# A third level of seven-product multiplication in more pairs of steps, and mixed kernels spread otherwise, in a fused AdaLN and FFN kernel

## The chip, the cores and the metric

One Trainium2 chip; the kernel runs on 1 of its cores. The metric is the device time of one execution in microseconds. Before the change: 2576.84 us, the median of three runs (2576.32 to 2578.92).

## The reference

All arrays are float32. x is (32, 128, 2048). Two blocks follow each other:

```
agg_w[b] = sum_k att[b,k] * weight[k]          # 32 mixed kernels of 128 x 128, att from a small MLP and a softmax
h   = agg_w[b] @ x[b] + agg_b[b]               # for every sample b
x1  = x + h @ W.T + bias + low-rank update     # W is 2048 x 2048, the update 16 experts of rank 16
y   = grouped conv of x1 along L (9 taps, 4 groups of 32 channels) + context + bias
t   = y[:, perm] in 16 heads of 128
out = x1 + (gelu(t @ up) @ down)[:, unperm]    # per head 128 -> 512 -> 128
```

What the change touches is the large product, x (4096 rows of 2048) by W (with the low-rank update added into it), and the 32 mixed kernels, which are made beside it on VectorE.

## The kernel before

The engines are named as in the profile: PE does matmuls, DVE is VectorE, ACT ScalarE, POOL GpSimd, and SP issues most DMAs.

**Three levels of seven products.** The large product is split into 2 x 2 blocks three times in the manner of Strassen and Winograd: seven products of sums and differences in place of eight.

- The outer level is a loop of seven *rounds*, `ROUNDS = P1, P2, P6, P7, P5, P3, P4`. Each has its own weights: four blocks of W, or differences of them (`outer_weights`), brought in and combined on POOL while the round before runs. What a round yields is added into partial sums in DRAM that are loaded before and stored after a step (`ADDED`, `olds_load`, `part_store`).
- A round has eight *steps* g = 0 to 7, each 512 rows of x. `multiply` does the inner level: seven products P1 to P7, each of four matmuls of 128 x 128 by 512 columns. Their second weights t1, t2, t4 are made by `inner_weights` on POOL, at step 7 of the round before; the sums `s` of the input by `x_combine` on POOL, one step ahead.
- The third level works on *pairs* of steps (g, g + 1). In a pair listed in `PAIRS`, the inner products P2 and P4 of both steps (16 matmuls of 512 columns) are done together as seven *quarters* of four matmuls of 256 columns each: `multiply_third`. The differences of the weights come from `third_weights` (half on POOL at once, half as `quarter_ops` on DVE, one between two products), the sums of the inputs (tile `sq`) from `third_inputs`, four operations on POOL, or on DVE in round P6.
- In a pair listed in `MORE`, P3 and P7 are done the same way as a second family: `multiply_more`. Only P1, P5 and P6 stay as full products. A quarter of the second family needs two additions on DVE, of 512 and of 256 elements, where one of the first needs one. `more_weights` makes eight differences on POOL and eight (`more_ops`) on DVE, `more_inputs` four sums (tile `sv`) on POOL. In such a pair four quarters come in the even step and ten in the odd one; the odd step's order is P1, two quarters, P5, two, P6, two, two, P3's, P4's.

Before the change MORE has the middle pairs, steps 2 to 5, of rounds P7 and P3; PAIRS has all pairs but the first of P1, and in P4 the first alone.

**Order.** The program is scheduled by hand: each engine does its instructions in the order in which the code gives them. `between(j)` is called after each product and puts other work of DVE there: two operations of a mixed kernel (`mixed_kernel`, L714; eight make one 128 x 128 kernel), one quarter_op and one more_op. In rounds P2 to P3 each of the steps 1 to 6 makes one mixed kernel. In round P1 `w_make_two` makes W with its update, two of its 16 blocks ahead of each of the first six steps, and `row_sums` and `unsummed_first` add up rows of W on DVE. `small` is a generator with the small MLP, which goes on by a little after each step.

**Buffers.** All large tiles of 8 KB a partition share 26 slots (`SLOTS`), taken in the order of the code; a new tile waits until the last reader of the slot's old one is done. PSUM has eight banks, used in turn by hand (`bank`, `done`). After the seven rounds, and partly beside P4, come mixing, convolution and the heads' FFN, which the change does not touch.

Of the kernel before, what the change touches and what calls it, by code (L numbers as in the profile page):

```python
# [11 lines left out]
ALU = mybir.AluOpType  # L12
# [36 lines left out]


PAIRS = {
    "P1": (1, 2, 3), "P2": (0, 1, 2, 3), "P6": (0, 1, 2, 3), "P7": (0, 1, 2, 3),
    "P5": (0, 1, 2, 3), "P3": (0, 1, 2, 3), "P4": (0,),
}
MORE = {"P7": (1, 2), "P3": (1, 2)}
ENDS = ("P1", "P4")
EARLY = 2

# [2 lines left out]
def adaln_ffn_kernel(  # L61
# [355 lines left out]
    def in_pair(r, g):  # L417
        return g // 2 in PAIRS[r]

    rest = []  # L420

    def third_inputs(i, eng):

        (x11, x12), (x21, x22) = (
            [xa[n][:, 1, :, h * NQ : (h + 1) * NQ] for h in range(2)] for n in (i, i + 1)
        )
        tt = eng.tensor_tensor
        t = slot(f"sq_{i}", (P, 4, 2, NQ))
        tt(t[:, 0], x21, x22, ALU.add)
        tt(t[:, 1], t[:, 0], x11, ALU.subtract)  # L430
        rest.append((t[:, 2], x11, x21))
        rest.append((t[:, 3], x12, t[:, 1]))
        if eng is nc.gpsimd:
            sums_rest(eng)
        return {
            "P1": x11, "P2": x12, "P3": t[:, 3], "P4": x22,
            "P5": t[:, 0], "P6": t[:, 1], "P7": t[:, 2],
        }

    def sums_rest(eng):  # L440
        while rest:
            eng.tensor_tensor(*rest.pop(0), ALU.subtract)

    def more_weights(name, rhs):

# [33 lines left out]
    def in_more(r, g):  # L479
        return g // 2 in MORE.get(r, ())  # L480

    def multiply_more(r, g, lhs, rhs, accs, between, families):

        px, py = bank(), bank()
        if g % 2 == 0:
            both = [accs]
            held.extend((both, {}, {}))
        both, *sums = held
        if g % 2:
            both.append(accs)  # L490

        def add(ps, *to):
            for si, oi in to:
                for acc in accs:
                    nc.vector.tensor_tensor(acc[:, si, oi], ps, acc[:, si, oi], ALU.add)  # L495

        def product(k, ps, first, last):
            for kc in range(4):
                nc.tensor.matmul(  # L499
                    ps, lhsT=lhs[k][:, bass.ts(kc, P)], rhs=rhs[k][kc],  # L500
                    start=first and kc == 0, stop=last and kc == 3, skip_group_check=True,
                )

        def quarter(n, k):

            quarters, x = families[n]
            qs = sums[n]
            if k in ("P1", "P5", "P2"):
                qs[k] = bank()
            ps = qs[{"P6": "P1", "P7": "P1", "P4": "P1", "P3": "P5"}.get(k, k)]  # L510
            first, last = k in ("P1", "P2", "P5"), k in ("P2", "P3", "P4")
            for i, out in enumerate(halves(ps)):
                for kc in range(2):
                    nc.tensor.matmul(  # L514
                        out, lhsT=x[k][:, 1 - i if n else i, bass.ts(kc, P)],
                        rhs=quarters[i][k][kc],
                        start=first and i == 0 and kc == 0, stop=last and i == 1 and kc == 1,
                        skip_group_check=True,
                    )
            b, h = {  # L520
                "P1": (0, 0), "P2": (0, 0), "P6": (0, 1), "P5": (1, 1), "P7": (1, 1),
                "P3": (0, 1), "P4": (1, 0),
            }[k]
            cols = slice(h * NQ, (h + 1) * NQ)
            for acc in both[b]:
                part = acc[:, :, n, cols]
                nc.vector.tensor_tensor(  # L527
                    part, ps.rearrange("p (s n) -> p s n", s=2), part, ALU.add
                )
                if n:  # L530
                    part = acc[:, 1, 0, cols]
                    nc.vector.tensor_tensor(part, ps[:, NQ : 2 * NQ], part, ALU.add)
            if last:
                done(ps)

        def quarters_of(*nks):
            if g % 2:
                for n, k in nks:
                    quarter(n, k)

        product("P1", px, True, False)
        add(px, (0, 0))
        between(0)
        quarters_of((0, "P6"), (0, "P5"))
        product("P5", py, True, True)
        add(py, (1, 1), (0, 1))
        done(py)
        between(1)
        quarters_of((1, "P6"), (0, "P7"))
        product("P6", px, False, True)  # L550
        add(px, (0, 1), (1, 1), (1, 0))
        done(px)
        between(2)
        if g % 2 == 0:
            quarter(0, "P1")
            quarter(0, "P2")
            between(3)
            quarter(1, "P1")
            between(4)
            quarter(1, "P2")  # L560
            between(5)
            return
        quarters_of((1, "P5"), (0, "P3"))
        between(3)
        quarters_of((1, "P7"), (0, "P4"))
        between(4)
        quarters_of((1, "P3"))
        between(5)
        quarters_of((1, "P4"))
        held.clear()  # L570
        for b, accs in enumerate(both):
            for (_, new), acc in zip(ADDED[r], accs):
                part_store(new, g - 1 + b, acc, nc.sync)
# [648 lines left out]
    for i, (r, g) in enumerate(steps):  # L1222
        ri = i // NG
        last_round = ri + 1 == len(ROUNDS)
        if i + 1 < len(steps):
            if i + 1 not in xs:
                xs[i + 1] = x_loads(*steps[i + 1])
            if not last_round:
                lhs[i + 1] = x_combine(*steps[i + 1], xs.pop(i + 1))
                if g == 2 * PAIRS[r][0]:  # L1230
                    quarters, quarter_ops = third_weights(r, rhs)
                if in_pair(r, g) and g % 2 == 0 and g > 0 and r != "P6":
                    sq = third_inputs(i, nc.gpsimd)
                    if in_more(r, g):
                        sv = more_inputs(i)
                if r in MORE and g == 2 * MORE[r][0] - 1:
                    more, more_ops = more_weights(r, rhs)
        if i == 0:
# [48 lines left out]
        def between(j):  # L1287

            if j == 3 and 0 <= k_early < EARLY:
                outer_sums(k_early, early_x)  # L1290

            b = (ri - 1) * (NG - 2) + g + 1 if ri > 0 else g - (NG - 2)
            if (g in range(1, NG - 1) if ri > 0 else g >= NG - 2) and b < B:
                k = j - 2 if r == "P5" and g == 1 else j
                if 0 <= k < KEXP // 2:
                    mixed_kernel(b, (2 * k, 2 * k + 1))
            if ri == 0 and j == 2:
                for k in blocks[6 + 2 * g : 8 + 2 * g]:
                    wt[k] = w_load(*k)
            if j < 4 and quarter_ops:  # L1300
                nc.vector.tensor_tensor(*quarter_ops.pop(0), ALU.subtract)
            if j < 4 and more_ops:
                nc.vector.tensor_tensor(*more_ops.pop(0), ALU.subtract)
            if i == NG - 1 and j == 3:
                olds_load(i + 1)
            if j == 3 and ahead and steps[i + 2][0] == "P6":
                xs[i + 2] = x_loads(*steps[i + 2])
            if ri == 0 and j in (1, 3) and unsummed:
                row_sums(*unsummed.pop())
            if ri == 0 and j == 5 and unsummed_first:  # L1310
                t = unsummed_first.pop(0)
                tt = nc.vector.tensor_tensor
                tt(wsum[:, 0, 0], wsum[:, 0, 0], t[:, 0, 0], ALU.add)
                tt(wsum[:, 0], wsum[:, 0], t[:, 1], ALU.add)
            if last_round:
                if j == 1 and i + 1 < len(steps):
                    lhs[i + 1] = x_combine(*steps[i + 1], xs.pop(i + 1))
                    olds_load(i + 1)
                if j == 4 and i + 2 < len(steps):
                    xs[i + 2] = x_loads(*steps[i + 2])  # L1320
                if j in (2, 4):
                    stage(k0 + j // 2, stage_first)
                if j % 2:
                    stage_third(k0 + j // 2)
                else:
                    stage(k0 + j // 2, stage_second)
# [10 lines left out]
            multiply(r, g, lhs.pop(i), rhs, olds.pop(i), between)  # L1337
        xa.pop(i - 1, None)
        ss.pop(i - 1, None)
        if in_pair(r, g) and g % 2 == 0 and (g == 0 or r == "P6" or last_round):  # L1340
            sq = third_inputs(i, nc.gpsimd if r in ENDS else nc.vector)
        next(chain, None)
        if i > 4:
# [95 lines left out]
```

## Time and profile before

| | |
|---|---|
| median of the runs | 2576.84 us |
| the profiled execution's own time | 2577.27 us |
| its span, first to last instruction | 2575.5 us |
| PE busy | 2564.0 us |
| DVE busy | 1579.5 us, 2450 instructions |
| POOL busy | 1394.2 us, 1158 instructions |
| matmul records | 7142, two for each matmul |
| mean granted TensorE clock | 0.999 |

The views used: the page (busy times of the engines; the chain of work that ended last, followed back from the last instruction to whatever released each), that chain in order of time (start, length, what; "x56" are 56 records of one line in a row), tables of busy time in stretches of the span, and the instructions of one engine in order of time, with its idle time before and what ended it in brackets. A line such as L594 is a product in `multiply_third` (L357 in `multiply`, L499 in `multiply_more`), L607 and L514 are the quarters of the two; L714 is a mixed kernel's operation, L283 an outer sum on POOL. Tile names come without numbers: `xt` is an input of the large product, `P_t`, `P_q`, `P_v` weights of the inner level and of the third level's two families.

Rounds as seen on PE: P1 from 33 to 297 us (with the making of W), P2 to 483, P6 to 669, P7 to 853, P5 to 1039, P3 to 1223; then P4 with the rest.

### The profile page before, as it was taken

Reading aid. Unit: us, or ns where it says so; the run is one execution under the profiler, and the core shown is the slowest. Engines: PE = TensorE matmul, PEld = TensorE weight load, DVE = VectorE, ACT = ScalarE, POOL = GpSimd, SP = SyncE. Lnnn points to the kernel's source line nnn. Section 1 sums busy time; section 2 is a strip of 40 time slices with the busy share of each in tenths; the row PEclk is TensorE's granted clock in tenths of the full one; section 3 lists DMA queues with packets and bytes.
Section 4 is the critical chain, followed back from the end, with each engine's and each line's share of the span. In section 5 each row is a group of like instructions: output and inputs, shape, how many; then the busy total and the mean of one; then the engine's idle time right before and its main releaser. Section 6 shows DMA issues by size and latency. Waiting matters only on the chain.

```text
span 2575.5 us, 22121 instructions
## 1 busy us (share of the span) xinstructions
PE 2564.0 (100%) x7142; PEld 1355.4 (53%) x7142; DVE 1579.5 (61%) x2450; ACT 532.3 (21%) x1099; POOL 1394.2 (54%) x1158
## 2 busy tenths in 40 slices
PE   9999999999999999999999999999999999999999
PEld 4455555555566555566554554455555554455543
DVE  5665576666585576675476666666666666667611
ACT  0000000000000000000011244444444444444432
POOL 7431788878997736989432134444344434434222
PEclk9999999999999999999999999999999999999999
DMA  7452588579366486574866887787777877777432
GB/s 322 182 211 113 198 338 344 212 285 370 151 249 263 196 337 273 221 287 168 281 230 210 279 290 266 224 259 230 226 223 234 252 246 223 222 251 237 164 123 90
DMA packets 186867, 610.42 MB, mean 237 GB/s; under 512 B 17664, under 2 KB 91904, under 8 KB 142336
## 3 DMA queue, kind: packets, MB, share of 16 engines
q1 hardware_dynamic: 147936, 473.48, 51.2%
q0 software_dynamic: 32992, 132.14, 15.2%
q10 hardware_dynamic: 5824, 3.40, 0.5%
q8 instruction: 57, 0.93, 0.1%
q14 instruction: 58, 0.48, 0.1%
HBM read 372.45 MB, written 202.94 MB: 223 GB/s over the span
## 4 chain that ended last, share of the span: by engine, by line
PE 95%; DVE 3%; DMA 2%; issue 0%; SPq 0%; POOLq 0%; ACT 0%; ACTq 0%; DVEq 0%
PE bank L594 26%; PE bank L986 17%; PE bank L997 17%; PE bank L607 9%; PE bank L357 7%; PE bank L842 6%; PE bank L750 4%; PE bank L499 3%; PE bank L223 3%; PE bank L514 2%; DMA w<-in_WT 1%; DVE ags L714 1%; DMA xt<-in_xT 0%; DVE u L527 0%; DVE u L495 0%
## 5 line engine op out<-in xcount | busy, mean ns | idle before, releaser
L986 PE MATMUL bank<-t,ws 128*128 128x512 f32 x1024 | 460.3, 592 | 0.0
L997 PE MATMUL bank<-gl,ws 128*128 128x512 f32 x1024 | 460.1, 592 | 0.0
L1004 POOL DMA_INDIRECT out<-t,orow x128 | 152.3, 1189 | 535.8 <-DVE t L1002 452.5
L989 ACT ACTIVATE gl<-bank 128x512 f32<-128x512 f32 x512 | 306.1, 598 | 433.3 <-PE bank L986 414.1
L997 PEld LDWEIGHTS bank<-gl,ws 128*128 128x128 f32 x1024 | 194.6, 190 | 232.9 <-issue 231.5
L986 PEld LDWEIGHTS bank<-t,ws 128*128 128x128 f32 x1024 | 194.6, 190 | 226.6 <-issue 222.2
L594 PE MATMUL bank<-P_t,s_P 128*128 128x512 f32 x640 | 284.3, 592 | 0.4 <-ACT m_P L589 0.4
L1002 DVE TENSOR_TENSOR t<-bank,t 128x512 f32<-128x512 f32 x128 | 88.4, 690 | 320.2 <-PE bank L997 309.4
L735 POOL TENSOR_TENSOR x<-x,fb 128x512 f32<-128x512 f32 x128 | 174.5, 1392 | 198.9 <-DMA x<-in_x 136.4
L741 ACT ACTIVATE bank<-w,aggb 128x512 f32<-128x512 f32 x128 | 80.8, 684 | 880.3 <-DMA w<-w_d 867.8
L283 POOL TENSOR_TENSOR xt<-xt,xt 128x512 f32<-128x512 f32 x120 | 159.0, 1358 | 104.6 <-DMA xt<-in_xT 88.4
L714 DVE SCALAR_TENSOR_TENSOR ags<-mix,att_bc,ags 128x128 f32<-128x128 f32 x224 | 195.5, 873 | 4.7
L594 PEld LDWEIGHTS bank<-P_t,s_P 128*128 128x128 f32 x640 | 121.4, 190 | 140.4 <-issue 136.6
L587 DVE TENSOR_TENSOR u<-bank,u 128x512 f32<-128x512 f32 x156 | 101.6, 686 | 147.4 <-PE bank L594 135.1
L594 PE MATMUL bank<-wo_P,s_P 128*128 128x512 f32 x416 | 184.7, 592 | 0.0
L319 POOL TENSOR_TENSOR s_P<-xt 128x512 f32<-128x512 f32 x52 | 68.8, 1323 | 204.0 <-DMA xt<-in_xT 164.2
L970 POOL DMA_INDIRECT t<-hx_d,row x128 | 131.1, 1025 | 56.6 <-issue 25.6
L587 DVE TENSOR_TENSOR p<-bank,p 128x512 f32<-128x512 f32 x96 | 64.6, 687 | 117.8 <-PE bank L594 117.1
L594 PEld LDWEIGHTS bank<-wo_P,s_P 128*128 128x128 f32 x416 | 79.0, 190 | 89.2 <-issue 87.3
L842 PE MATMUL bank<-va,tw_l 128*128 128x256 f32 x512 | 121.5, 380 | 0.7 <-DVE va L826 0.7
L853 ACT ACTIVATE cv<-bank,ctxb 128x128 f32<-128x128 f32 x256 | 73.0, 368 | 234.6 <-PE bank L842 234.6
L753 DVE TENSOR_TENSOR x<-bank,x 128x512 f32<-128x512 f32 x128 | 88.1, 690 | 50.8 <-POOL x L735 21.9
(242 smaller groups left out, 3869.0 us busy)
## 6 DMA issues: line engine op xcount, KB each, us to landing
xt<-in_xT SPq DMA_DIRECT2D x84, 1024.0 KB
u<-u_d SPq DMA_DIRECT2D x40, 1024.0 KB
wo_P<-wb_d SPq DMA_DIRECT2D x36, 1024.0 KB
u<-c_d SPq DMA_DIRECT2D x64, 512.0 KB
x<-in_x SPq DMA_DIRECT2D x32, 1024.0 KB
xg<-x SPq DMA_DIRECT2D x256, 128.0 KB
hx_d<-x1t SPq DMA_DIRECT2D x32, 1024.0 KB
hx_d<-ht SPq DMA_DIRECT2D x32, 1024.0 KB
```

The costliest lines, as they stand in the source:

```text
L283: nc.gpsimd.tensor_tensor(out[:, i, j], a[:, i, j], b[:, i, j], op)
L357: nc.tensor.matmul(ps, lhsT=lhs[k][:, bass.ts(kc, P)], rhs=rhs[k][kc], start=first and kc == 0, stop=last and kc == 3, skip_group_check=True,)
L587: nc.vector.tensor_tensor(to, ps, to, ALU.add)
L594: nc.tensor.matmul(ps, lhsT=lhs[k][:, bass.ts(kc, P)], rhs=rhs[k][kc], start=first and kc == 0, stop=last and kc == 3, skip_group_check=True,)
L607: nc.tensor.matmul(out, lhsT=sq[k][:, i, bass.ts(kc, P)], rhs=quarters[i][k][kc], start=first and i == 0 and kc == 0, stop=last and i == 1 ...
L714: nc.vector.scalar_tensor_tensor(ag, mix[:, k], att, ag, ALU.mult, ALU.add)
L735: nc.gpsimd.tensor_tensor(xt[:, f], xt[:, f], late["fb"][:, f], ALU.add)
L842: nc.tensor.matmul(out, lhsT=w[:, 2 * i + r], rhs=rhs, start=first and r == 0, stop=last and r == 1, skip_group_check=True,)
L986: nc.tensor.matmul(pu, lhsT=w[:, m * P : (m + 1) * P], rhs=t[:, 0], start=True, stop=True)
L989: nc.scalar.activation(gl[m], pu, AF.Gelu)
L997: nc.tensor.matmul(pd, lhsT=w[:, (MC + m) * P : (MC + m + 1) * P], rhs=gl[m], start=(m == 0), stop=(m == MC - 1),)
L1004: nc.gpsimd.indirect_dma_start(out=out, out_offset=bass.IndirectOffsetOnAxis(ap=orow[:, g, h : h + 1], axis=0), in_=t[:, 1], in_offset=None,)
```

## The change

- `PAIRS`: P1's first pair gets the third level. So `third_weights` of P1 comes two steps sooner, and P1's steps 0 and 1 go through `multiply_third` in place of `multiply`. Its DVE part, `quarter_ops`, starts at step 1.
- `MORE`: round P6 gets the second family in steps 2 to 5, and P7 and P3 in their last pair too, steps 6 and 7.
- In P6 the sums `sq` of such a pair stay on DVE: two at the end of the even step, two after the first quarters of the odd one. `sums_rest` takes operations with their kind and a count.
- Mixed kernels: in the rounds of MORE their 48 operations are handed out over steps 1 to 7, one after each of the first four products in steps 2 and 4 and two in the others, in place of two in steps 1 to 6. The other rounds keep theirs.
- In round P1 the row sums of W are moved: one of the sums of step 1 to step 2, and those of the first four blocks from the ends of steps 0 to 3 to steps 2 (twice), 3 and 4.

```diff
 PAIRS = {
-    "P1": (1, 2, 3), "P2": (0, 1, 2, 3), "P6": (0, 1, 2, 3), "P7": (0, 1, 2, 3),
+    "P1": (0, 1, 2, 3), "P2": (0, 1, 2, 3), "P6": (0, 1, 2, 3), "P7": (0, 1, 2, 3),
     "P5": (0, 1, 2, 3), "P3": (0, 1, 2, 3), "P4": (0,),
 }
-MORE = {"P7": (1, 2), "P3": (1, 2)}
+MORE = {"P6": (1, 2), "P7": (1, 2, 3), "P3": (1, 2, 3)}
...
-    def third_inputs(i, eng):
+    def third_inputs(i, eng, later=False):
...
-        tt(t[:, 0], x21, x22, ALU.add)
-        tt(t[:, 1], t[:, 0], x11, ALU.subtract)
-        rest.append((t[:, 2], x11, x21))
-        rest.append((t[:, 3], x12, t[:, 1]))
+        rest.append((t[:, 0], x21, x22, ALU.add))
+        rest.append((t[:, 1], t[:, 0], x11, ALU.subtract))
+        if not later:
+            sums_rest(eng, 2)
+        rest.append((t[:, 2], x11, x21, ALU.subtract))
+        rest.append((t[:, 3], x12, t[:, 1], ALU.subtract))
...
-    def sums_rest(eng):
-        while rest:
-            eng.tensor_tensor(*rest.pop(0), ALU.subtract)
+    def sums_rest(eng, n=4):
+        for _ in range(min(n, len(rest))):
+            eng.tensor_tensor(*rest.pop(0))
...
         quarters_of((0, "P6"), (0, "P5"))
+        if g % 2:
+            sums_rest(nc.vector)
         product("P5", py, True, True)
...
+        if g == 0:
+            b = (ri - 1) * (NG - 2) + 2
+            mixes = [(b + n // KEXP, n % KEXP) for n in range((NG - 2) * KEXP)]
+            mixes = [m for m in mixes if m[0] < B]
...
-                if in_pair(r, g) and g % 2 == 0 and g > 0 and r != "P6":
-                    sq = third_inputs(i, nc.gpsimd)
-                    if in_more(r, g):
-                        sv = more_inputs(i)
+                if in_pair(r, g) and g % 2 == 0 and g > 0:
+                    if r != "P6":
+                        sq = third_inputs(i, nc.gpsimd)
+                    elif in_more(r, g):
+                        sq = third_inputs(i, nc.vector, True)
+                if in_more(r, g) and g % 2 == 0:
+                    sv = more_inputs(i)
...
-            if (g in range(1, NG - 1) if ri > 0 else g >= NG - 2) and b < B:
+            if (g in range(1, NG - 1) if ri > 0 else g >= NG - 2) and b < B and r not in MORE:
                 k = j - 2 if r == "P5" and g == 1 else j
                 if 0 <= k < KEXP // 2:
                     mixed_kernel(b, (2 * k, 2 * k + 1))
+            if r in MORE and 0 < g and j < 4:
+                for _ in range(1 if g in (2, 4) else 2):
+                    if mixes:
+                        b, k = mixes.pop(0)
+                        mixed_kernel(b, (k,))
...
-            if j < 4 and quarter_ops:
+            if i and j < 4 and quarter_ops:
...
-            if ri == 0 and j in (1, 3) and unsummed:
+            if ri == 0 and unsummed and (j in (1, 3) and (i, j) != (1, 3) or (i, j) == (2, 4)):
                 row_sums(*unsummed.pop())
-            if ri == 0 and j == 5 and unsummed_first:
+            if (i, j) in ((2, 0), (2, 5), (3, 0), (4, 0)) and unsummed_first:
...
-        if in_pair(r, g) and g % 2 == 0 and (g == 0 or r == "P6" or last_round):
+        if in_more(r, g) and r == "P6":
+            sums_rest(nc.vector, 2)
+        elif in_pair(r, g) and g % 2 == 0 and (g == 0 or r == "P6" or last_round):
             sq = third_inputs(i, nc.gpsimd if r in ENDS else nc.vector)
```

## The prediction

> **What bounds the kernel now.** I read the page first (busy times, then the chain that ended last), then the chain in order of time for what a product costs, then a table of busy times by stretches, then the instructions of DVE and POOL in time.
>
> ```profile
> PE 2564.0 (100%) x7142; PEld 1355.4 (53%) x7142; DVE 1579.5 (61%) x2450; ACT 532.3 (21%) x1099; POOL 1394.2 (54%) x1158
> ...
> PE 95%; DVE 3%; DMA 2%; issue 0%; SPq 0%; POOLq 0%; ACT 0%; ACTq 0%; DVEq 0%
> ```
>
> PE has work in 2564.0 of 2575.5 us and makes up 95% of the chain: a matmul taken away shortens the program by its own time, unless something else is then late. So I need the price of a product and a list of what may be late.
>
> ```profile
> 82.11 24.03 PE bank L357 x56
> ...
> 220.25 17.17 PE bank L594 x40
> 237.41 12.10 PE bank L607 x56
> ...
> 762.10 10.30 PE bank L499 x24
> 772.40 6.91 PE bank L514 x32
> ```
>
> This is the chain in order of time (start, length, what). Each product is two records. 56 records with 512 columns take 24.03 us, 0.429 us each; 56 records with 256 columns take 12.10 us, 0.216 us each. Half the columns cost half, with the weight load hidden both times.
>
> [...]
>
> **PE: what goes.** A plain pair of steps is 2 x 24.03 = 48.06 us. A pair with the third level on P2 and P4 is 2 x 17.17 + 12.10 = 46.44 us: 16 full products became 28 halves. A pair with the third level on P3 and P7 as well is 44.77 us when nothing waits (762.10 to 806.87 in the same chain). So P1's first pair gives 1.62 us, and each of the four new pairs (two of P6, the last of P7 and of P3) gives 1.67 us: 1.62 + 4 x 1.67 = 8.3 us. The instructions to check it by: 5 x 12 products more, so 7142 + 120 = 7262 matmul records.
>
> **DVE: what the new pairs add.** Seven more additions of 512 (0.6 us apart) and seven of 256 (0.33 us apart) in each of the four pairs, 6.5 us a pair; in P6 also 8 differences of 256 for the weights. The waits that exist are in such pairs:
>
> ```profile
> core 0: us, PE busy (x) PEld busy (x) DVE busy (x) ACT busy (x) POOL busy (x), PEclk, DMA share, GB/s
> ...
> 576.50:622.90 46.40, 46.40 (x137) 25.84 (x136) 29.36 (x39) 0.00 (x0) 39.02 (x32) 1.00 0.94 364
> ...
> 715.80:761.90 46.10, 45.25 (x161) 30.21 (x160) 43.06 (x53) 0.00 (x0) 45.47 (x37) 1.00 0.63 254
> 761.90:806.70 44.80, 44.80 (x161) 30.41 (x161) 30.04 (x49) 0.00 (x0) 35.74 (x30) 1.00 0.73 284
> ```
>
> These are P6's third pair and P7's second and third. The second pair of P7 lasts 46.1 us and not 44.8: DVE is busy in 43.06 of it. The chain shows how a wait is made:
>
> ```profile
> 757.81 1.30 DVE ags L714
> 759.11 0.60 DVE u L527
> 759.72 0.34 DVE u L532
> 760.06 0.04 issue
> 760.10 1.99 PE bank L514 x8
> ```
>
> The last quarter, P4, adds into the bank that P7's quarter used; P7's additions (L527, L532) stand on DVE behind two operations of a mixed kernel (L714), and PE waits. Those are slow only while POOL works. With POOL idle two of them took 0.73 us, with POOL busy 2.76:
>
> ```profile
> 525.75 2.76 DVE L714 SCALAR_TENSOR_TENSOR ags<-mix,att_bc,ags 128x128 f32<-128x128 f32 x2
> ...
> 537.77 0.73 DVE L714 SCALAR_TENSOR_TENSOR ags<-mix,att_bc,ags 128x128 f32<-128x128 f32 x2
> ```
>
> In the four pairs of today the waits of PE are 1.4, 0, 0.3 and 1.0 us (46.1, 44.8, 45.1 and 45.8 us against 44.8): 2.7 in all. The new order of mixed kernels puts 4 operations and not 8 into steps 2 and 4, some 3 to 5 us of DVE at 0.7 to 1.3 each; that should clear the wait in the middle of P7's second pair (0.7 us, an addition late behind that backlog). It doesn't touch steps 3, 5 and 7, where the wait at the end arises, and two operations still stand before P7's additions. P6's pairs: DVE 29.4 + 6.5 less four operations is 33 of 44.8 us, in the second pair some 6 more for the weights' differences; P7's last: 17.75 + 6.5 + about 8 for a mixed kernel moved to step 7 is 32. All lie between pairs of today that wait 0 and 1.0. I take 0.55 for each of eight pairs, 4.4 in place of 2.7: **+1.7 us**. The ends are 0 (as P7's third pair) and 1.4 (as its second) for each, so -2.7 to +8.5.
>
> **POOL and the buffers in P6 and P7.** P6 gains 8 differences of 256 (0.73 us) and 8 operations of 512 (1.27 us) on POOL, 16 us. Two gaps can take them:
>
> ```profile
> 549.20 11.31 POOL L283 TENSOR_TENSOR xt<-xt,xt 128x512 f32<-128x512 f32 x8 [18.34 <-DMA xt<-in_xT]
> ...
> 599.11 10.89 POOL L283 TENSOR_TENSOR xt<-xt,xt 128x512 f32<-128x512 f32 x8 [6.59 <-PE bank L607]
> ...
> 674.27 5.83 POOL L283 TENSOR_TENSOR xt<-xt,xt 128x512 f32<-128x512 f32 x4
> ```
>
> The bracket is idle time before. 11 us (weights, first `sv`) fall into the 18.34, the second `sv` (5.1) into the 6.59. From 599 to 771 POOL then works without a gap, as now, while PE comes 1.62 + 2 x 1.67 = 5.0 us sooner. The tightest place is P7's second step: its input is ready at 680.1 (674.27 + 5.83) and PE starts on it at 686.5, 6.4 us later. After the change 1.4 us are left. So the gaps cover the added work, by little; I cost it at **0**. Without that cover the added 16 us would come against 25 us of idle and 6.4 of lead. A second thing sits there: three more of the 26 slots are taken (two weight tiles, `sv`), so the loads of x for steps 5 to 7 wait for later releases, behind POOL's reads among others, in stretches where the DMA engines are 85% and 94% busy. By the releases of today, moved by three places, the load for step 7 lands some 0 to 5 us after POOL wants it. Bounds: -1 (loads start earlier, because the stores ahead of them on SP follow PE) to +6.
>
> **P1's first pair.** Added: 4 operations on POOL (5 us), and the eight differences for the weights come two steps sooner, 6 to 9 us ahead of two stores, in a stretch where POOL then sat idle 18.94 us for a load. On SP the store of step 0 goes away, behind which the next loads stand today. The loads of W for the third making come later for want of slots, by about 20 us by my count, 4 us before they are needed. Five additions more on DVE; the row sums moved off the step ends where PE waited 0.2 and 0.6 us. Taken as **0**, ends -0.9 and +4.
>
> **Turn of the rounds.** With the last pair of P7 and of P3 at the full third level, two weight tiles and `sv` live until the pair's end, just when the next round's weights (`inner_weights`) want three slots. Today the third of them waits 4.52 us on POOL. By the releases of that pair the second would wait until the P5 product has read its tile, 834, the third until P6's, 841 in place of 831: POOL's row shifts by 10 us, and the first use, with 4 us (P5's tile, fourth block, 851 against 857.5) to spare, holds. **0**, ends 0 and +9 a turn.
>
> **Sum.** -8.3 + 1.7 = -6.6 us. The profiled execution took 2577.27 us (span 2575.5 and 1.8 around it): 2570.7. It lies 0.4 above the median of the runs, 2576.84; taken from the median, 2570.2. I say **2570.4**.
>
> **Rivals.**
> A. POOL and the slots in P6 take most of it: the late load of step 7 puts POOL behind, P7's second step waits, and P6's pairs wait 1.4 each. For: POOL 98% busy from 623 to 762, DMA at 94%. Against: the two gaps, and x for steps 2 to 4 is loaded ahead of the squeeze. Price: 8.3 less 1.7, 2 x 0.8 more and 4 to 8 gives a change of -1 to +3; with milder waits -5: 2572 to 2580.
> B. Slower: at the turns P7 to P5 and P3 to P4 the new weights' second tile is not free until the pair's end. POOL's 16 operations (20 us) then start with the round; the fourth block's first tile comes 13 us after the end, and PE wants it after 6, and behind it input and quarter weights are late: 8 to 10 us a turn, 16 to 20 in two, 8 to 12 net: 2585 to 2589. It decides when the tile frees later than about 845, 7 us before the pair's end. Against: the P5 product frees a tile at 834.
> C. It does better: the spread clears all waits in the new pairs and P1: -8.3 - 2.7 - 0.9: 2565.
>
> **Chances.** The forecast with its milder neighbours and C: 0.62. A: 0.24. B and like it: 0.14. A measurement here tells about 0.2% from no change, 5.2 us: faster means below 2571.7, slower above 2582.0. So faster 0.62, same 0.24, slower 0.14. The range runs from near C, 2566, to the end of A, 2580.
>
> **What would show it.** 7262 matmul records; four new pairs of about 45.3 us, the first pair of P1 at 46.4 and a making of 12; waits of PE only before the last quarters. A is seen in POOL rows after 599 without a gap and PE waiting for POOL `xt` or `s_P` at P6's last or P7's second step; B in POOL waiting over 15 us before a weight tile of P5 or P4. I would be wrong if halves cost more than half in P6, or if a load's landing, not DVE, ends the waits.

## The result, and the profile after

The changed kernel takes 2586.2 us (2584.6 to 2587.8, seven runs) where the kernel before takes 2577.0: 1.0034 of it, interval 1.0024 to 1.0044. It is **slower by 9 us**, 16 us from the forecast. The profiled execution took 2587.75 us, its span is 2585.9.

The same two lines of the page as shown of before (busy times, and the shares of the chain that ended last):

```profile
PE 2561.8 (99%) x7262; PEld 1381.4 (53%) x7262; DVE 1624.7 (63%) x2519; ACT 532.2 (21%) x1099; POOL 1431.6 (55%) x1186
...
PE 93%; POOL 3%; DVE 2%; DMA 2%; issue 0%; POOLq 0%; ACT 0%; ACTq 0%; SPq 0%; DVEq 0%
```

The 7262 records are there and PE is busy for 2.2 us less, yet PE's share of the chain fell from 95 to 93%: POOL has 3% that it did not have. The table by stretches, for P1's first pair with the making of W that stands in it, P6's two new pairs, P7's third and last, and P3's last:

```profile
core 0: us, PE busy (x) PEld busy (x) DVE busy (x) ACT busy (x) POOL busy (x), PEclk, DMA share, GB/s
46.20:104.70 58.50, 58.50 (x166) 31.18 (x165) 31.59 (x38) 5.97 (x9) 38.53 (x36) 1.00 0.41 157
533.90:579.10 45.20, 44.97 (x161) 30.27 (x160) 35.08 (x54) 0.00 (x0) 33.54 (x27) 1.00 0.84 328
579.10:637.00 57.90, 47.31 (x161) 31.95 (x161) 35.76 (x49) 0.00 (x0) 47.08 (x38) 0.91 0.77 291
...
774.80:820.40 45.60, 45.04 (x162) 30.31 (x161) 31.08 (x45) 0.00 (x0) 37.39 (x31) 1.00 0.72 279
820.40:865.30 44.90, 44.90 (x162) 30.35 (x161) 33.33 (x49) 0.00 (x0) 39.07 (x32) 1.00 0.43 167
...
1188.20:1233.00 44.80, 44.80 (x162) 30.30 (x161) 33.67 (x49) 0.00 (x0) 38.87 (x32) 1.00 0.38 144
```

All but one of these are what the forecast said (58.5 is a pair of 46.4 and a making of 12.1). **P6's steps 4 and 5 take 57.9 us**, with 10.6 us in which PE is idle and a granted clock of 0.91. The waits of that place (engine, line, releaser, us in total, times, longest):

```profile
PE bank L516 <- DVE sq L444: 10.6, 1, 10.6
DVE sq L444 <- POOL wo_P L283: 9.3, 1, 9.3
```

DVE stands before writing the sums `sq`, and what ends its wait is not an input: it is POOL's combination of two tiles of outer weights, which `sq` doesn't read. The chain there (start, length, what):

```profile
577.47 8.40 DMA xt<-in_xT
...
586.02 5.00 POOL xt L283 x4
...
600.89 1.26 POOL sv L475
602.16 4.89 POOL wo_P L283 x4
607.05 0.02 issue
607.07 1.74 DVE sq L444
...
610.53 5.56 PE bank L516 x14
```

The x of step 5 was summed by 591.0; PE wanted `sq` at 599.8; DVE was free at 597.8. But `sq` was given the buffer slot of the second tile of the outer weights, and that is free only when POOL has combined them, behind `s`, `sv` and all else in its row, at 607.0. 14 records of 256 columns then take 5.56 us, 0.40 each and not 0.216: after the idle the matmuls run at half rate, with a granted clock of 0.50 from 610.5 to 613.0 us.

The second place is the fourth making of W in P1:

```profile
134.28 0.69 DVE m_P L591
134.98 0.99 DVE wsum L243
135.97 4.90 DMA w<-in_WT
...
140.99 0.70 DVE w L226
141.69 0.04 issue
141.74 8.28 PE bank L223 x12
```

The load of the second block stood on SP until 135.97, for a slot (before the change it went out at 111.7). SP's own waits name what held it: the store of a finished block of W (`wb_d<-w`), for 24.3 us. The load landed at 140.9; PE had been at that making since 134.3. The 12 records take 0.69 us each and not 0.429; the granted clock is 0.50 from 141.7 to 147.0 us.

To add this up I take, for each matmul record, the time to the next one's start less 0.429 or 0.216 us, and call the sum **excess**: what PE loses to waits and to the clock. Before 10.7 us, after 29.1, 18.4 more: P6 13.1 (10.75 of waiting, 2.4 at half rate), P1's making 5.8 more (waits 3.0, half rate 2.9), the start 0.9, the rest less than before. 18.4 - 8.3 of products saved is 10.1; the span grew by 10.4.

### The profile page after: what moved, and what is told of

Read it like the earlier page. It is cut to its first block, busy times and chain, and to the rows that moved or that the text cites. A ratio compares the mean times of both kernels' runs of the same rounds, so it can differ in the third digit from the quotient of the medians.

```text
span 2585.9 us, 22456 instructions
## 1 busy us (share of the span) xinstructions
PE 2561.8 (99%) x7262; PEld 1381.4 (53%) x7262; DVE 1624.7 (63%) x2519; ACT 532.2 (21%) x1099; POOL 1431.6 (55%) x1186
## 4 chain that ended last, share of the span: by engine, by line
PE 93%; POOL 3%; DVE 2%; DMA 2%; issue 0%; POOLq 0%; ACT 0%; ACTq 0%; SPq 0%; DVEq 0%
PE bank L598 21%; PE bank L990 17%; PE bank L1001 17%; PE bank L611 7%; PE bank L846 6%; PE bank L516 6%; PE bank L357 5%; PE bank L501 5%; PE bank L754 4%; PE bank L223 3%; POOL xt L283 1%; DMA xt<-in_xT 1%; PE bank L180 1%; DVE ags L718 1%; POOL wo_P L283 0%
## 5 line engine op out<-in xcount | busy, mean ns | idle before, releaser
L598 PE MATMUL bank<-P_t,s_P 128*128 128x512 f32 x544 | 241.4, 592 | 0.4 <-ACT m_P L593 0.4
L718 DVE SCALAR_TENSOR_TENSOR ags<-mix,att_bc,ags 128x128 f32<-128x128 f32 x224 | 204.9, 915 | 4.3
L598 PEld LDWEIGHTS bank<-P_t,s_P 128*128 128x128 f32 x544 | 103.3, 190 | 120.6 <-issue 116.5
L591 DVE TENSOR_TENSOR u<-bank,u 128x512 f32<-128x512 f32 x132 | 85.3, 686 | 96.0 <-PE bank L598 92.9
L598 PE MATMUL bank<-wo_P,s_P 128*128 128x512 f32 x288 | 127.8, 592 | 0.0
L846 PEld LDWEIGHTS bank<-va,tw_l 128*128 128x128 f32 x512 | 97.2, 190 | 41.6 <-issue 30.1
L754 PE MATMUL bank<-u,agl 128*128 128x512 f32 x256 | 115.1, 592 | 0.0
```

The lines of the kernel that those rows point to most:

```text
L598: nc.tensor.matmul(ps, lhsT=lhs[k][:, bass.ts(kc, P)], rhs=rhs[k][kc], start=first and kc == 0, stop=last and kc == 3, skip_group_check=True,)
L718: nc.vector.scalar_tensor_tensor(ag, mix[:, k], att, ag, ALU.mult, ALU.add)
L754: nc.tensor.matmul(pm, lhsT=ag, rhs=u[:, f], start=False, stop=True, skip_group_check=True)
L846: nc.tensor.matmul(out, lhsT=w[:, 2 * i + r], rhs=rhs, start=first and r == 0, stop=last and r == 1, skip_group_check=True,)
```

## The experiments

Each is a kernel of its own, run in five rounds against the kernel before on the same chip (e15 in three), given as a ratio to it with its interval. The table has the excess of the profiled execution, in us, up to 20 us (the start, which differs between these executions and is left out of the argument), from there to 160 (the makings of W) and from 500 to 720 (P6 and P7's first steps):

| kernel | ratio (95%) | start | P1 | P6 to P7 |
|---|---|---|---|---|
| before | 1 | 2.2 | 1.2 | 0.6 |
| after | 1.0034 (1.0024 to 1.0044) | 3.1 | 6.4 | 14.3 |
| e1 P6's first pair only | 0.9989 (0.9980 to 0.9998) | 3.0 | 4.6 | 1.2 |
| e2 oldest rows first | 1.0023 (1.0014 to 1.0032) | 3.4 | 4.3 | 13.4 |
| e3 sq's slot early | 1.0011 (1.0002 to 1.0020) | 3.6 | 5.2 | 7.9 |
| e4 last pairs alone | 0.9992 (0.9983 to 1.0001) | 2.4 | 0.7 | 0.4 |
| e5 rows back | 1.0020 (1.0011 to 1.0029) | 3.2 | 2.0 | 14.7 |
| e6 e1 and rows back | **0.9981** (0.9972 to 0.9990) | 3.4 | 1.3 | 1.1 |
| e7 e3, x of step 7 first | 1.0000 (0.9991 to 1.0009) | 3.1 | 4.7 | 6.2 |
| e8 e7 and rows back | 0.9992 (0.9983 to 1.0001) | 3.6 | 1.4 | 6.1 |
| e9 before, 25 slots | 1.0026 (1.0015 to 1.0036) | 2.2 | 8.3 | 0.7 |
| e10 before, 24 slots | 1.0117 (1.0102 to 1.0133) | 2.8 | 9.7 | 0.7 |
| e11 combination first | 1.0003 (0.9994 to 1.0012) | 2.9 | 1.3 | 9.1 |
| e12 e8, sv on DVE | 0.9999 (0.9990 to 1.0008) | 3.2 | 1.4 | 5.7 |
| e13 P6's second pair only | 1.0029 (1.0019 to 1.0039) | 2.3 | 1.3 | 13.0 |
| e14 P6's first and last | 1.0006 (0.9997 to 1.0015) | 2.6 | 1.4 | 9.5 |

**e1.**
```diff
-MORE = {"P6": (1, 2), "P7": (1, 2, 3), "P3": (1, 2, 3)}
+MORE = {"P6": (1,), "P7": (1, 2, 3), "P3": (1, 2, 3)}
```


> The changed kernel, with the second family in P6's steps 2 and 3 alone; steps 4 and 5 are a plain third-level pair again. Theory (slots): the 13.4 us lost in steps 4 and 5 come from the sums sq of step 4, which get their buffer slot only after POOL's combination of the outer weights has released it (10.75 us of idle PE, then 2.6 us of matmuls at half rate). Without the family there two tiles fewer are wanted: 2586.2 - 13.4 + 1.7 (the saving of that pair) = 2574.5 us. Rival (POOL's work): the 11 us of weight differences and first sums that POOL still does in P6, out of 16, keep it behind; then some 11/16 of the loss stays, near 2578 to 2583, and POOL stands ahead of a wait elsewhere in P6.

Measured 2574.6: the theory's number. P6's excess falls from 14.3 to 1.2, with 11 of the 16 us of added POOL work still in P6. One pair costs nothing there; these 11 us of POOL's work are not the loss.

**e2.**
```diff
-                row_sums(*unsummed.pop())
+                row_sums(*unsummed.pop(0))
```


> The changed kernel, with the row sums taking the oldest block of W that is left and not the newest; as many operations at the same places. Theory (slots): the fourth making of W waited since its second block's load stood on SP until 135.97, for a slot; with the oldest block summed first, a slot comes free at about 125, the load lands before 137.3 where PE wants it, and the 6.5 us there go (2.1 + 0.9 of waiting and 3.4 of matmuls at half rate): 2579.7. Rival (DVE's work, the moved sums delay what follows them on DVE): nothing changes, 2586.

Measured 2583.7: between the two. The load went out at 125.5, and the wait for it, 0.9 us, is gone: with the oldest block summed first, the slot is one whose store had long landed, and it comes free when DVE's sum ends. But 2.1 us stay, and the chain shows whose they are:

```profile
135.22 1.14 DVE wsum L243
...
136.39 1.22 DVE wsum L243
137.61 0.61 DVE wsum L1329
...
139.39 0.70 DVE w L226
140.09 0.04 issue
140.13 6.26 PE bank L223 x10
```

DVE adds the rows that the change moved here (L243, 2.5 us), then the first blocks (L1329, which stood here before as well), and only then takes the making's first product off its bank. So P1 has two causes: the slot, and DVE's moved work just ahead of the making. Both expectations were half right.

**e3.**
```diff
+        if later:
+            nc.vector.memset(t[:, 0, 0, 0:1], 0.0)
         rest.append((t[:, 0], x21, x22, ALU.add))
```


> The changed kernel, where in P6 one element of sq is set by DVE as soon as the sums are planned, so that sq takes its slot two steps of the code sooner, ahead of the loads; the sums stay where they were, POOL's work is the same. Theory (slots): sq gets the slot of an x tile whose last reader is done at 575, the sums run at 597 when DVE has them, PE goes on at 599.8 without a wait, and the clock doesn't drop: 2586.2 - 13.4 = 2572.8. A load of x for step 6 then waits in sq's stead, until about 607, landing at 615 where POOL wants it at about 612 and PE at 624. Rival (POOL's work): sv is ready no sooner than 602 and x for step 5 no sooner than 591, POOL is behind, and no more than 5 us come back: 2581 or above.

Measured 2580.7. Slots are given in the order of first use, so one element set early is enough: PE's wait for `sq` falls from 10.75 to 1.1 us, with POOL's work untouched. It was the slot. Yet only 6 of 13 us came back (by the time alone it is next to the rival's 2581: POOL is late as well, only at a later place), since a second wait had been hidden behind the first (POOL's instructions, idle time in brackets):

```profile
621.86 4.99 POOL L283 TENSOR_TENSOR wo_P<-wo_P,wo_P 128x512 f32<-128x512 f32 x4
634.47 10.13 POOL L283 TENSOR_TENSOR xt<-xt,xt 128x512 f32<-128x512 f32 x8 [7.61 <-DMA xt<-in_xT]
```

The load of x for step 7 takes the slot that this combination has just released: it can't go out before 626.9, and its whole landing time stands on POOL's row. POOL then makes P7's weights too late; PE waits 3.2 us and loses 1.8 at half rate (granted clock 0.96 from 670 to 715 us).

**e4.** PAIRS, P6 and the row sums as before; from the change only the last pairs of P7 and P3, and the mixed kernels' order.
```diff
-MORE = {"P6": (1, 2), "P7": (1, 2, 3), "P3": (1, 2, 3)}
+MORE = {"P7": (1, 2, 3), "P3": (1, 2, 3)}
```


> One part of the change alone: the second family in the last pairs of P7 and P3 and the mixed kernels spread; P1's first pair, P6 and the row sums as before. If the two places above are the whole loss: two pairs at 1.67 us less, with waits at the pairs' ends as many as before, 2577.0 - 3.3 = 2573.7. Rival (the turns of the rounds are late, the weight tiles of the next round wait): 8 us a turn, above 2585.

Measured 2575.5 against 2577.8, 2.2 us less; 3.3 lies within the interval, and so does 0; what the two pairs save is seen in the table of the changed kernel, 44.9 and 44.8 us where they took 46.4. No wait at the turns of the rounds.

**e5.** Both conditions of the row sums as before the change.
```diff
-            if ri == 0 and unsummed and (j in (1, 3) and (i, j) != (1, 3) or (i, j) == (2, 4)):
+            if ri == 0 and j in (1, 3) and unsummed:
                 row_sums(*unsummed.pop())
-            if (i, j) in ((2, 0), (2, 5), (3, 0), (4, 0)) and unsummed_first:
+            if ri == 0 and j == 5 and unsummed_first:
```


> The changed kernel with the row sums of W where they were before the change; P1's first pair keeps its third level. The run with the oldest rows first kept 2.1 us of waiting at the fourth making of W, though its load landed early: what PE waited for there is DVE, which had the moved sums (2.5 us of rows and 1.9 of first blocks) just ahead of the making. Theory (the moved sums, in two ways: DVE's time 2.1 us, the slot of the oldest block 0.9 us, and 3.3 us of matmuls at half rate that follow the idle): all of it goes, waits of 0.2 to 0.6 us at the ends of steps come back: 2586.2 - 6.3 + 0.6 = 2580.5. Rival (the early third level in P1 is what crowds out the load and DVE): some 3 us or less come back, 2583 or above.

Measured 2583.0, by its number the rival's; but in P1 the theory holds: PE doesn't wait at the fourth making at all; 1.3 us of small waits come back at 66.7 and 97.1. P1's excess falls by 4.4, not 5.7. So the moved sums, not the early third level, cost P1 most of its time (2.0 us of excess are left, against 1.2 before).

**e6.** e1 and e5 together.


> As the run before, and P6 with the second family in steps 2 and 3 alone: P1's first pair, one pair of P6, the last pairs of P7 and P3. If the two places are all that the change loses, what is left is 1.6 + 1.67 + 3.3 = 6.6 us off the kernel before, with as many waits as before: 2577.0 - 6.6 = 2570.4, better than either kernel. If P1's early third level has its price in another place, 2573 to 2576.

Measured 2572.7 against 2577.6, better than both kernels: 4.9 us less than before, of 6.6 by products. The start is 1.2 us worse in the profiled execution, and P6's pair and what follows wait some 1.4 more.

**e7.**
```diff
-        if ahead and steps[i + 2][0] != "P6":
+        if ahead and (steps[i + 2][0] != "P6" or steps[i + 2][1] in (7,)):
             xs[i + 2] = x_loads(*steps[i + 2])
```


> The run with sq's slot taken early, and in P6 the loads of x for step 7 ahead of the loads of the last outer weights on SP; nothing else moves. In that run POOL stood 7.6 us before x of step 7, whose load took a slot that POOL's own combination of outer weights had just released; after it POOL came 3.2 us late with P7's weights, and 2.1 us of matmuls at half rate followed. Theory (loads that get a slot from POOL's last work put their landing time on POOL's chain): with two of the three loads 11 us sooner POOL starts on x some 5 us sooner, the wait at P7's first step goes: 5.3 us less than that run, about 2575. Rival (POOL's added work itself makes it late): POOL is late at P7's weights again by 2 us or more, 2578 to 2581.

Measured 2577.7, between the two. POOL's 7.6 us before step 7 are gone, but it stands 5.7 us before the next load, x of P7's first step. PE waits 1.4 and 1.8 us for P7's weights, and no half rate follows: the granted clock is 1.00 from 670 to 715 us.

**e8.** e7 and e5 together.


> The run before with the row sums back in their old places: the whole change but for these, with both slots mended. By the theories 8.3 us of matmuls are saved and the waits are about as many as before, with 1 us in P6's second pair: 2577.0 - 8.3 + 1 = 2569.7. If POOL is still late at P7's weights, 2572 to 2575.

Measured 2575.4: P1 is well, P6 keeps 5 us more than e6. With the second pair and all mends it is slower than e6 without that pair.

**e9 and e10.** The kernel before.
```diff
-SLOTS = 26
+SLOTS = 25
```


> The kernel before with 25 slots in place of 26, nothing else. Theory (the buffers were at their limit before the change, so each further tile that lives costs a wait): slower, by 1 to 6 us, seen as POOL or PE waiting for a load (DMA xt or w) that SP issued late, in P6 or P1 first. Rival (the slots had room, and what the change lost is POOL's and DVE's added work): 2577, within 1 us.

> The kernel before with 24 slots in place of 26. Theory (slots): worse than with 25; in P6, where two weight tiles and sv cost the changed kernel 13.4 us, some 5 to 15 us, 2582 to 2592. Rival (room): 2577 to 2579.

2583.3 and 2606.2 us. One slot less costs 6.4 us, and it costs them where the change lost its smaller part, at the fourth making of W (chain of e9):

```profile
133.33 6.12 DMA wb_d<-w
...
139.52 4.97 DMA w<-in_WT
...
144.61 0.70 DVE w L226
145.31 0.04 issue
145.35 4.72 PE bank L223 x6
```

The load waits until the store of an older block has read its slot. P1 had no slot to spare. In P6, against what I had expected, PE waits in neither: the kernel before had room for two tiles there, and what breaks it is the third, or that with POOL's 16 us. That was not separated. The second run also went far past what I had expected of it: of the 26 us by which its profiled execution is longer, some 8.5 lie up to 160 us, 11 from there to 500 and 8 after 1300.

**e11.**
```diff
+        if r == "P6" and g in (4,):
+            for k, combine in waiting.items():
+                nxt[k] = combine()
+            waiting = {}
         if i + 1 < len(steps):
```


> The changed kernel with the row sums back; in P6's step 4 POOL combines the waiting outer weights ahead of the sums of x and not behind them, so that it releases their slot, which sq takes, some 20 us sooner. sq is planned where it was, no element is set early. Theory (sq waits for a slot that POOL's order holds): the 10.7 us of idle and the 2.9 us at half rate go, and as in the run where sq took its slot early 3 to 5 us come back at P7's weights through the late load of x for step 7: 2582.5 - 13.6 + 5 = 2574. Rival (POOL is simply behind by its added work, whatever the order): x for step 5 comes 5 us later and PE waits for it, 2578 or above.

Measured 2577.7 against 2577.0. The wait for `sq` goes this way too (0.7 us left), by POOL's order alone. POOL again stands 8.6 us before x of step 7 and is late at P7's weights: 3.9 us of waiting, 3.2 at half rate, some 2 us more than I had put on it.

**e12.** e8, where `sv` of P6's second pair is made by DVE after `sq`; one element set by DVE keeps its slot where it was taken.
```diff
-                tt = nc.gpsimd.tensor_tensor
...
+            rest_v.extend(ops)
...
+            while rest_v:
+                nc.vector.tensor_tensor(*rest_v.pop(0))
```


> The run with all mends (sq's slot early, x of step 7 first, row sums back), and the four sums sv of P6's second pair on DVE and not on POOL: 5.9 us of POOL's work less there. In that run POOL was still 1.5 and 1.8 us late at P7's weights, after standing 5.7 us before a load of P7's x. Theory 1 (POOL's work and the releases behind it): POOL and all loads that wait for it come up to 5.9 us sooner, both waits go: 2575.3 - 3.3 = 2572. Theory 2 (that last load was slow because seven transfers stood together on the DMA engines): POOL waits for it as long as before, 2575.

Measured 2576.4: theory 1 falls. With 5.9 us less to do POOL waits 6.5, 2.7 and 3.8 us for loads of x and is nearly as late as in e8 (1.3 and 1.4 us at P7's weights, there 1.5 and 1.8). The DMA share (second last number) shows what goes with it, first e12, then before:

```profile
595.00:604.50 9.50, 8.55 (x32) 5.66 (x31) 8.29 (x14) 0.00 (x0) 2.99 (x3) 1.00 0.81 336
604.50:612.30 7.80, 7.80 (x30) 5.37 (x29) 6.28 (x10) 0.00 (x0) 7.77 (x7) 1.00 0.00 0
612.30:625.00 12.70, 12.25 (x49) 8.95 (x48) 9.54 (x15) 0.00 (x0) 10.58 (x9) 1.00 0.93 341
625.00:652.00 27.00, 27.00 (x79) 14.55 (x77) 18.73 (x26) 0.00 (x0) 21.90 (x18) 1.00 0.99 383
```

```profile
595.00:604.50 9.50, 9.50 (x33) 5.92 (x32) 6.74 (x11) 0.00 (x0) 5.39 (x4) 1.00 1.02 428
604.50:612.30 7.80, 7.80 (x30) 5.37 (x29) 4.39 (x7) 0.00 (x0) 7.40 (x8) 1.00 0.92 354
612.30:625.00 12.70, 12.70 (x40) 7.30 (x39) 7.62 (x10) 0.00 (x0) 12.70 (x11) 1.00 0.82 314
```

The wait of 6.5 us comes first, for a load issued at 585.7 that lands at 602.1. After it the DMA engines do **nothing for 7.8 us** in the middle of P6, whose steps 4 and 5 have a DMA share of 0.94 in the kernel before: SP's next load has no slot until POOL has read x, at 612.3. From 612.3 the share is 0.93, from 625 to 652 it is 0.99, and a load of x issued at 627.60 lands 23.79 us later; the 2.7 and 3.8 us are waits for loads after that gap. So POOL waits for loads that wait for POOL, and with less to do it only waits longer. That the transfer time lost in such gaps is what holds it back is argued, not shown by a run of its own; but the gap goes with the loss. From 600 to 625 us the DMA share is 0.87 to 0.96 in the kernel before, e1, e4 and e6, and 0.52 to 0.69 in each kernel that has the family in P6's second or last pair.

**e13 and e14.** The row sums as before, P6 with other pairs.
```diff
-MORE = {"P6": (1, 2),
+MORE = {"P6": (2,),
```
and `(1, 3)` in e14.

> The changed kernel with the row sums back and the second family in P6's steps 4 and 5 alone (not 2 and 3). As many tiles live there as in the whole change, but sv of steps 2 and 3 and the early weights don't come before it, and by the order of the slots sq gets one that a store releases, not POOL. Theory (it is which slot sq gets): no wait of 10 us at step 5; x of step 7 still takes the slot of POOL's last combination and comes late, so 2572 to 2575. Rival (steps 4 and 5 can't have the family, whatever stands before): 2580 or above.

> The changed kernel with the row sums back and the second family in P6's steps 2, 3, 6 and 7. Steps 4 and 5, where x, two tiles of outer weights and sums want slots at once, are plain; but sv of step 6 puts 5 us on POOL just ahead of P7's weights. Theory (slots and late loads in the middle are the loss, POOL has lead at the end): 2577.0 - 8.3 + 1 = 2570. Rival (POOL has no lead left at P7's weights, whatever the slots): 3 us of waiting or more there, with matmuls at half rate after it, 2574 to 2577.

2584.4 and 2578.6. By the times my theory fails in both; the rivals hold, e14 even past its 2577. In e13 `sq` waits for no slot, as the theory said, but x of step 7 does, as in e3: its last load goes out when POOL's combination ends (628.9), POOL stands 8.5 us before it, and PE, sooner than in e3, waits 5.4 us, with 3.1 at half rate. So in none of the orders tried do steps 4 and 5 have room for the family. In e14 the middle is better, though the two weight tiles stay in use across it, but POOL is late at P7's weights (waits of 1.0 and 3.3 us, 1.8 at half rate). Of the sets tried, steps 2 and 3 alone cost nothing; steps 0 and 1 and the last pair by itself were not tried.

**e15.** The kernel before, with idles of PE made on purpose.
```diff
+        if (r, g) in IDLE:
+            pw = bank()
+            nc.tensor.matmul(pw[0:2, 0:4], lhsT=wsc, rhs=cs, start=True, stop=True)
+            for _ in range(IDLE[r, g]):
+                nc.scalar.mul(wsc[0:2], pw[0:2, 0:2], 0.0)
+            nc.tensor.matmul(pw[0:2, 0:4], lhsT=wsc, rhs=cs, start=True, stop=True)
+            done(pw)
```


> The kernel before, with PE made to idle on purpose at eight steps of P2, P5 and P3: a small matmul, then 2, 5, 7, 9, 11, 13, 16 and 20 small operations on ACT that read its result, then a small matmul that reads theirs. It measures what an idle of PE costs beyond itself. From the runs so far: after idles of 1.1, 1.4 and 1.8 us the next matmuls kept their pace, after 2.1 us or more they ran at half rate, for 1.3 to 3.4 us of lost time. Theory (the clock drops when the idle is longer than about 2 us): no half rate after the short ones, 1 to 3.4 us lost after each longer one, not growing with the length. Rival (those half rates belong to what the program did there, making W or waiting for POOL): none of these idles is followed by slow matmuls.

Measured 2623.0. The theory holds for these eight idles. Excess of the matmuls in the some 10 us after each idle, in order of length (0.2 is what any such stretch has; the 7.0 us were two operations only, but they stood on ACT behind an operation of `small`, L1123, that waited for DVE until 348.8):

| idle, us | 1.25 | 1.63 | 2.41 | 2.80 | 3.38 | 4.15 | 6.21 | 7.02 |
|---|---|---|---|---|---|---|---|---|
| excess after it, us | 0.2 | 0.2 | 2.0 | 2.0 | 2.0 | 2.6 | 2.8 | 2.2 |

By stretches (PEclk is the third number from the end), the idles of 1.63 and 2.41 us and what follows:

```profile
446.40:448.10 1.70, 0.23 (x5) 0.12 (x4) 1.64 (x5) 1.13 (x7) 1.70 (x3) 1.00 0.00 0
448.10:458.00 9.90, 9.90 (x25) 4.48 (x25) 3.88 (x8) 0.00 (x0) 5.33 (x5) 1.00 0.96 333
967.70:970.10 2.40, 0.16 (x3) 0.05 (x2) 2.33 (x4) 1.78 (x11) 0.00 (x0) 1.00 0.00 0
970.10:971.20 1.10, 1.09 (x5) 0.58 (x6) 0.15 (x1) 0.00 (x0) 0.00 (x0) 1.00 0.75 313
971.20:974.60 3.40, 3.40 (x6) 1.41 (x5) 0.00 (x0) 0.00 (x0) 0.00 (x0) 0.53 0.98 400
```

## Why the prediction was wrong

- **The products (-8.3): right.** 7262 records; the new pairs of P7 and P3 take 44.9 and 44.8 us. A half costs half, in P6 too where the granted clock is 1.00 (8 records of 256 columns from 619.79 to 621.51 us, 0.215 each).
- **DVE's waits at pair ends (+1.7): too high.** Over 0.15 us there are 0.40, 0.73 and 0.93, 2.1 us in eight pairs, against 2.3 by the same count before in four. The spread mixed kernels cleared the wait in the middle of P7's second pair, as said.
- **POOL and the buffers in P6 (0, ends -1 and +6): the step that failed, with 13.1 us.** What I had named as fatal, that a load's landing and not DVE ends the waits, came only in part: it ends 0.9 us in P1 and the waits behind the first one in P6 (e3, e11). The large wait in P6 is for a slot, which I had not named. The step asked which *loads* come late when three more slots are taken. It had that right in kind (the load of step 7, "0 to 5 us after POOL wants it", stood 7.6 us late once nothing hid it, e3). It left out that a tile that an *engine* writes takes a slot too: `sq` got the one released last, by an instruction far down POOL's row. And it took POOL's idle of 18.3 us as cover for work, while by e12 a POOL with less to do only waits longer for its loads.
- **P1 (0, ends -0.9 and +4): wrong too, by 5.2 us.** I named the third making as the tight one; it was the fourth, whose load came 24 us later: with the sums moved it got a slot that a store still read until 135.90 (e2, with the oldest block summed first, got one at 125.5). And I counted the moved row sums as a gain at the old places (0.2 and 0.6 us), not as 2.5 us of DVE at the new one, just ahead of a making (e2, e5).
- **The turns (0): right.** No wait at 865 or 1233, though the working has a slip: its 851 and 857.5 are 6.5 us apart, not 4. Rival B's number was met by luck, by no part of its mechanism.
- **Rival A** named P6, POOL and the slots, at 4 to 8 us; e3 and e11 show its course (5 to 7 us) behind the larger wait, only that PE waits for P7's weights in the first step and not for the input of the second.
- **Left out of every price:** what an idle of PE costs beyond itself. Of the 18.4 us of further excess 5.3 are matmuls at half rate, after idles of 3.0 (2.1 and 0.9, close together) and 10.75 us.

What is shown: the slot of `sq` (e3, e11 take that wait away by two ways), the moved row sums (e2, e5), and that POOL stays late in P6 with the second pair whatever was mended (e7, e8, e11, e12, e13). What stays open: whether the third tile or POOL's added time tips P6, and whether the lost transfer time is its price.

## What to carry to other kernels

Where tiles share a pool of buffers, list for each new tile which old one it replaces and what releases that, the tiles that engines write as well as those that are loaded; a releaser that stands late in an engine's row is a wait (here 9.3 us of DVE and 10.6 of PE). Where the DMA engines are nearly full, as in P6 here (share 0.94 from 576.5 to 622.9 us in the kernel before), look for loads that must wait for a compute engine's last read: in e12 they left the DMA engines idle for 7.8 us. That this lost transfer time is what held POOL back there was argued, not shown. And price a wait of PE with what follows it: here those of 1.25 to 1.8 us cost only themselves (e7, e15), those of 2.1 us and more (e2, e3, e15) some 1 to 3 us more.

## What the runs showed of the hardware

- After idles of PE of 1.4 and 1.8 us in e7 the granted clock stayed at 1.00 (670 to 715 us), and so it did after those of 1.25 and 1.63 us in e15 (399.7 to 410.0 and 448.1 to 458.0). After the idle of 2.41 us in e15 it was 0.53 from 971.2 to 974.6 and 0.98 from there to 980.0; after the wait for `sq` in P6 of the changed kernel it was 0.50 from 610.5 to 613.0, and 1.00 from 615.4 to 618.0.
- At a granted clock of 0.50 matmuls of 512 columns started 0.853 us apart where 0.429 is normal (changed kernel, the four starts from 142.75 to 145.31 us).
- The loss beyond the idle was some 1 to 3 us and grew little with its length: in e15 2.0 us after 2.41, 2.8 after 6.21, 2.2 after 7.02; 2.4 after the 10.75 in P6 of the changed kernel.
- The lower clock began after the end of some of these idles and within others. In e15 it was still 1.00 from 970.1 to 971.2, when work had gone on after the 2.41 us; in the idle of 4.15 us it was 0.75 (1211.7 to 1215.8) and after it 0.50 (1215.8 to 1220.0); in the wait for `sq` it was 0.50 from 607.0 to 610.5. What sets its begin and its end, and how short an idle suffices, is not shown.
- A load of 1 MB of x took 8.40 us from issue to landing in the changed kernel (issued at 577.47 us, DMA share 0.95 meanwhile), and in e12 16.36 us (issued at 585.72, shares of 0.94 and 0.81) and 23.79 us (issued at 627.60, share 0.99).
